# Two attention layers on 8 images: conv weights loaded a head at a time, the closing of a sum moved one unit ahead, first loads of the second pass moved into the first

## The chip, the cores and the metric

One NeuronCore of a Trainium2 chip runs one program that computes both layers for all 8 images. The metric is the time of one execution on the device, in microseconds (us). The kernel before took 4076.93 us, the median of 3 runs (4073.89 to 4082.44). Everything is float32.

## The reference

The input x has shape (8, 256, 64, 64). Layer 0 is an attention whose keys and values come from a 4x4 convolution of stride 4 with a normalization over channels; it runs in the kernel's first pass, and the change touches only where its buffers lie. Layer 1 is a linear attention on several scales, cut here to what matters:

```python
qkv = einsum('oc,bchw->bohw', w_qkv, x)                    # 768 channels
dw  = conv(qkv, w_dw, 5x5, padding 2, one group per channel)
agg = einsum('goi,bgihw->bgohw', w_pw, dw in 96 groups of 8)
ms  = concatenate([qkv, agg], axis=1)                      # 64 heads of 3 x 8 channels
q, k, v = relu(ms[..., :8]), relu(ms[..., 8:16]), ms[..., 16:]   # a column of ones is added to v
kv  = einsum('bhnd,bhne->bhde', k, v)                      # a sum over all pixels
out = einsum('bhnd,bhde->bhne', q, kv);  att = out[..., :-1] / (out[..., -1:] + 1e-15)
result = x + batchnorm(w_proj @ att)
```

## The kernel before, in words

`kernel_body` (L1440) calls three passes one after another; they share DRAM tensors and take their on-chip buffers from pools of their own. Pools of a later pass come to lie over pools of an earlier one, so a first use of a buffer can have to wait for the last use of what lay there. A scheduler orders the instructions of each engine from the program's order and its dependences, and it moves instructions past others where it can. All DMAs are issued by SP, one after another, and an issue that has to wait holds up those behind it.

**First pass** (`first_pass`, L575): layer 0, image by image, and w_qkv of its result. It writes to DRAM: x2 (layer 0's result), planes (qkv cut into grids of even and odd rows and columns), k and v with pixels on partitions, and wt, the 5x5 convolution and w_pw folded into matrices (`conv_weights`, L633).

**Second pass** (`second_pass`, L956): the heads of agg. It has 64 units u = (t, k, b): t of 2 halves, k of 4 groups of heads, b of 8 images, the image innermost, so that eight units in a row use the same weights. Each unit has two convolutions, what = 1 (its output, k, has pixels on partitions) and what = 0 (q, channels on partitions), each of three parts of 16 matmuls (`convolve`, L1070 and L1074). Part 2 comes first; its PSUM bank is copied to "both" by ScalarE (L1077). Parts 0 and 1 are added to "both" by VectorE (s, L1085), and ScalarE makes r by a ReLU (L1086). The matmul operands c come from the grids d by differences (`paired`: VectorE L1012 and L1013, and for what = 1 a copy on POOL, L1016). Further steps:

- `positive` (L1051): ReLU of kq on ScalarE (L1053), and a sum over it on POOL (`reduced`, L1046 to L1048).
- `summed_raw` (L1089): 64 matmuls give the k-by-v sums of the qkv heads in the bank "raw" (L1095). There is one such bank. `ended_raw` (L1138) adds the column for the sum of k by one matmul (L1142), and VectorE copies the bank to mraw (L1144, L1145), which is stored.
- `summed` (L1105): the sums of the agg heads (128 matmuls, L1112), weighted with taps (L1122, L1124) and mixed (L1127 to L1130); `ended` and `spread` bring them into the block form bd.
- `applied` (L1177): ng from r of q and bd, for two parities (L1182), then den (ScalarE L1184, VectorE L1185), tok (L1187), its transpose att (L1194) and the store of att to DRAM (L1196).

The loop runs these for four units at a time, one stage apart: raw and what = 1 of u, sums of u - 1, what = 0 of u - 2, ng of u - 3. In the program's order, `ended_raw(u - 1)` stands between parts 0 and 1 of `convolve(u, 1)`. Loads: grids by `load_cells` (L984, 578 KB each), kq and vq by `load_tokens` (L991, 512 KB; L1001, four of 384 KB), and weights by `load_weights` (L977), 1536 KB in one DMA:

```python
        if now and units[u][2] == 4 and u + 4 < n_all:
            load_weights(u + 4, 1)
        if conv and units[q][2] == 4 and q + 4 < n_all:
            load_weights(q + 4, 0)
```

**Third pass** (`third_pass`, L1246): the qkv heads' own attention and the projection. It loads constants first, the 128x128 mask msk (L1261), vec (L1332) and wproj (L1334); kvm is msk times the stored sums (L1274, L1280); n (L1358), den (L1360, L1361) and tok (L1363), a transpose by matmul (L1376, L1377), the projection p (L1394) of those and of the stored att of the second pass (agg, L1310). raw (L1290) and xs (L1299) are its other loads.

Of the kernel before, what the change touches and what calls it, by code (L numbers as in the profile page):

```python
# [27 lines left out]
F32 = mybir.dt.float32  # L28
# [4 lines left out]
P = 128  # L33
C = 256
# [8 lines left out]
D1 = 8  # L43
# [531 lines left out]
def first_pass(ctx: ExitStack, tc: tile.TileContext, a, fine, planes, x2d, kd, vd, wtd):  # L575
# [3 lines left out]
    const = ctx.enter_context(tc.tile_pool(name="const", bufs=1))  # L579
    nilpool = ctx.enter_context(tc.tile_pool(name="nilpool", bufs=1))  # L580
    xpools = [ctx.enter_context(tc.tile_pool(name=f"xpool{i}", bufs=1)) for i in range(2)]
    two = ctx.enter_context(tc.tile_pool(name="two", bufs=2))
    psum = ctx.enter_context(tc.tile_pool(name="psum", bufs=1, space=bass.MemoryType.PSUM))

    def bank(name):
# [46 lines left out]

    def conv_weights():  # L633
        for j in (2, 3, 0, 1):
            wd = two.tile([P, 16, 6, 16], F32, tag="wd", name=f"wd_{j}", bufs=1)
            nc.sync.dma_start(wd[:, :, :4], a.w_big[:, j].rearrange("p g (n f) -> p g n f", n=4))

            nc.vector.tensor_add(wd[:, :, 4:], wd[:, :, 0:4:2], wd[:, :, 1:4:2])
            for i in range(8):
                w = two.tile([P, 2, 6 * 16, D1], F32, tag="wb", name=f"wb_{j}_{i}", bufs=1)  # L640
                gs = slice(2 * i, 2 * i + 2)
                nc.vector.tensor_tensor(
                    w,
                    wd[:, gs].rearrange("p g n f -> p g (n f)").unsqueeze(3).to_broadcast([P, 2, 6 * 16, D1]),
                    consts["wsmall"][:, j, gs].unsqueeze(2).to_broadcast([P, 2, 6 * 16, D1]),
                    ALU.mult,
                )
                nc.sync.dma_start(wtd[j][:, gs], w.rearrange("p g n o -> p g (n o)"))
                yield
# [3 lines left out]

    def keys_values(b):
        xt = x_tiles[b]
        ln = lambda name: two.tile([P, 2, NK], F32, tag="ln", name=f"{name}_{b}", bufs=3)
        xr = ln("xr")

        ps = psum.tile([P, QB], F32, tag="sr", name=f"sr_{b}").rearrange("p (o k) -> p o k", o=2)
        taps = sorted((phase(dy, dx), dy * R + dx) for dy in range(R) for dx in range(R))  # L660
        for f, tap in taps:
            w = two.tile([P, 2, C], F32, tag="wsr", name=f"wsr_{b}_{f}", bufs=4)
            nc.sync.dma_start(w, a.w_sr[:, :, tap])
            for ci in range(2):
                for oc in range(2):
                    nc.tensor.matmul(  # L666
                        ps[:, oc],
                        w[:, ci, oc * P : (oc + 1) * P],
                        xt[:, ci, f * NK : (f + 1) * NK],
                        start=(f == ci == oc == 0),  # L670
                        stop=(f == R * R - 1 and ci == 1),
                        skip_group_check=True,
                    )
            yield
# [113 lines left out]
    def normed(b, s, c):  # L788
        av, den = sums["av"], sums["den"]
        i = 2 * ((b * NG + s) * 2 + c)  # L790
        att = two.tile([P, QB], F32, tag="att", name=f"att_{b}_{s}_{c}", bufs=4)
        r = two.tile([P, QB], F32, tag="rden", name=f"rden_{b}_{s}_{c}")
        nc.scalar.copy(att, av)
        nc.vector.reciprocal(r, den)  # L794
        nc.vector.tensor_mul(att, att, r)
        nc.scalar.activation(den, den, AF.Copy, accum_out=seen[:, i : i + 1])
        nc.scalar.activation(den, r, AF.Copy, accum_out=seen[:, i + 1 : i + 2])
        return att
# [10 lines left out]


    def new_stage(b, s):
        st = two.tile([P, 4, 2, NB + 1, NB + 1], F32, tag="stage", name=f"stage_{b}_{s}")
        row, col = (0 if s // 4 else NB), (0 if s // 2 % 2 else NB)
        v = st.rearrange("p j f y x -> p (j f) y x")
        nc.gpsimd.memset(v[:, :, row], 0.0)
        nc.gpsimd.memset(v[:, :, :, col], 0.0)
        return st
# [8 lines left out]
    def qkv(b, s, st, j):  # L826
# [16 lines left out]
        if j < 2:  # L843
            return
        if al == 0:
            turned[j] = two.tile([P, NB // 2, 4, D0], F32, tag=f"turned{j}", name=f"turned_{b}_{s}_{j}", bufs=1)
        t = turned[j]
        nc.vector.transpose(  # L848
            t[:, :, 2 * al : 2 * al + 2].rearrange("p y f e -> p f y e"),
# [106 lines left out]
def second_pass(ctx: ExitStack, tc: tile.TileContext, a, planes, kd, vd, wtd, kvd, attd):  # L956
    nc = tc.nc
    B = a.x.shape[0]
    const = ctx.enter_context(tc.tile_pool(name="const2", bufs=1))
    late = ctx.enter_context(tc.tile_pool(name="late2", bufs=2))  # L960

    data = [ctx.enter_context(tc.tile_pool(name=f"data2_{i}", bufs=1)) for i in range(3)]
    two = ctx.enter_context(tc.tile_pool(name="two2", bufs=2))
    psum = ctx.enter_context(tc.tile_pool(name="psum2", bufs=1, space=bass.MemoryType.PSUM))

    def bank(tag, name, bufs=1, n=512):
# [3 lines left out]
    n_all = len(units)  # L970
    wt, grids, cells, kqs, vqs = {}, {}, {}, {}, {}

    def load_weights(u, what):
        t, k, b = units[u]
        pool = data[k % 2 if what else 2]
        w = pool.tile([P, 4, 6 * P], F32, tag=f"w{what}_{k % 2}", name=f"w{what}_{t}_{k}")
        nc.sync.dma_start(w, wtd[2 * what + t][:, 4 * k : 4 * k + 4])  # L977
        wt[t, k, what] = w

    def load_cells(u, what):  # L980
        t, k, b = units[u]
        pool = data[u % 2 if what else 2]
        d = pool.tile([P, 4, (NB + 1) ** 2], F32, tag=f"d{what}_{u % 2}", name=f"d{what}_{u}")
        nc.sync.dma_start(d, planes[b, 2 * what + t][4 * k : 4 * k + 4].rearrange("g p e -> p g e"))  # L984
        grids[u, what] = d.rearrange("p g (y x) -> p g y x", x=NB + 1)


    def load_tokens(u):
        t, k, b = units[u]
        kq = data[u % 2].tile([P, 2, 4, P], F32, tag=f"kq_{u % 2}", name=f"kq_{u}")  # L990
        nc.sync.dma_start(  # L991
            kq.rearrange("p a c e -> p a (c e)"),
            kd[b][4 * t + k].rearrange("a y (m i) b e -> (y m) a (i b e)", i=2),
        )
        kqs[u] = kq
        vq = data[min(u % 3, 1)].tile([P, 4, 6 * P], F32, tag=f"vq_{u % 3}", name=f"vq_{u}")
        v = vd[b][4 * t + k]
        row = (NB2 + 2) * P
        for r in range(4):
            src = [[2 * row, NB], [4 * P, NB // 2], [1, 6 * P]]  # L1000
            nc.sync.dma_start(vq[:, r], bass.AP(tensor=v.tensor, offset=v.offset + r * row, ap=src))  # L1001
        vqs[u] = vq.rearrange("p r (c f h e) -> p r c f h e", c=6, f=4, h=4)
# [2 lines left out]

    def paired(u, what):
        d = grids[u, what]
        pool = two if what else late
        c = pool.tile([P, 2 + what, 4, (NB + 1) * NB // 2], F32, tag=f"c{what}", name=f"c{what}_{u}")
        v = c.rearrange("p n g (y x) -> p n g y x", x=NB // 2)  # L1010
        d0, d1, d2 = (d[:, :, :, i : i + NB - 1 : 2] for i in range(3))
        nc.vector.tensor_sub(v[:, 0], d0, d1)  # L1012
# [3 lines left out]
            nc.gpsimd.tensor_copy(v[:, 2], d1)  # L1016
        cells[u, what] = c

    load_weights(0, 1)
    load_cells(0, 1)  # L1020
    load_tokens(0)

    def load(src, name):
        t = const.tile(list(src.shape), F32, tag=name, name=name)
        nc.sync.dma_start(t, src)
        return t

    load_cells(1, 1)
    load_cells(0, 0)
    load_weights(0, 0)  # L1030
    taps = load(a.w_taps, "taps")
    mix = load(a.w_mix, "mix")
    msk = load(a.mask_h, "msk")
    rep_w = load(a.replicate, "rep_w")
    pix = load(a.pixel, "pix")
    ones = const.tile([P, 1], F32, tag="ones", name="ones")
    nc.vector.memset(ones, 1.0)
    eps = late.tile([P, 1], F32, tag="eps", name="eps", bufs=1)
# [3 lines left out]


    def reduced(u, what, t):
        r = two.tile([P, 4, P], F32, tag=f"red_{what}", name=f"red_{what}_{u}", bufs=1)
# [12 lines left out]
    def convolve(u, what, i):  # L1058
# [14 lines left out]
                        out = out.rearrange("p (y x) -> p y x", y=NB)  # L1073
                    nc.tensor.matmul(out, m, x, start=(da == 0), stop=(da == 1))  # L1074
        if i == 2:
            both = two.tile([P, QB], F32, tag="both", name=f"both{what}_{u}")
# [100 lines left out]
    def applied(u, par):  # L1177
# [2 lines left out]
        pn = bank("ng", f"ng_{u}_{par}", 1, 1024).rearrange("p (h n) -> p h n", h=4)  # L1180
        for h in range(4):
            nc.tensor.matmul(pn[:, h, : P + 16], q[:, par, h], bd[:, h], start=True, stop=True)  # L1182
        den = two.tile([P, 2, 4, 16], F32, tag="den", name=f"den_{u}_{par}")
        nc.scalar.activation(den[:, 0], pn[:, :, P : P + 16], AF.Identity, bias=eps)  # L1184
        nc.vector.reciprocal(den[:, 1], den[:, 0])  # L1185
        tok = two.tile([P, 16, D0], F32, tag="tok", name=f"tok_{u}_{par}")
        nc.vector.tensor_tensor(  # L1187
            tok.rearrange("p f (h e) -> p h f e", e=D1),
            pn[:, :, :P].rearrange("p h (f e) -> p h f e", e=D1),
            den[:, 1].unsqueeze(3).to_broadcast([P, 4, 16, D1]),  # L1190
            ALU.mult,
        )
        att = two.tile([P, 512], F32, tag="att", name=f"att_{u}_{par}")
        nc.vector.transpose(att, tok.rearrange("p f e -> p (f e)"))  # L1194
        c0 = P * t + D0 * k
        nc.sync.dma_start(attd[b][c0 : c0 + D0, par].rearrange("c j n -> j c n"), att)  # L1196
# [2 lines left out]
    for u in range(n_all + 3):  # L1199
# [16 lines left out]
            paired(u + 1, 1)  # L1216
        if now:
            convolve(u, 1, 0)
        if was:
            ended_raw(p)  # L1220
        if now:
            convolve(u, 1, 1)
        if u + 2 < n_all:
            load_cells(u + 2, 1)
# [10 lines left out]
            spread(p)  # L1235
        if conv:
            convolve(q, 0, 1)
        if now and units[u][2] == 4 and u + 4 < n_all:
            load_weights(u + 4, 1)
        if conv and units[q][2] == 4 and q + 4 < n_all:  # L1240
            load_weights(q + 4, 0)

# [338 lines left out]
```

## Time and profile before

| | |
|---|---|
| median of 3 runs | 4076.93 us (4073.89 to 4082.44) |
| the profiled execution | 4078.39 us |
| its span in the profile | 4076.5 us |
| mean granted clock of TensorE | 0.986 |
| first, second, third pass (by TensorE's work) | 0 to 2137, 2137 to 3422, 3422 to 4070 us |
| busy: TensorE, VectorE, ScalarE, POOL | 97%, 47%, 41%, 29% of the span |
| DMA | 691.31 MB, mean 170 GB/s |

The profile is of one execution. Times are counted from the start of its span. A row of a group of instructions gives line, engine, operation and tiles with counts and times. A row of the waits gives the engine, the line that waited, what let it go, and then the sum of the waiting in us, how often, and the longest. A row of the order of time gives start, duration, engine, line and operation; in brackets stands the idle time of the engine before it and what ended it. A table of stretches gives, for each stretch, its length, the busy time of TensorE, its weight loads, VectorE, ScalarE and POOL with the number of instructions, the clock that TensorE was granted, the share of time in which the 16 DMA engines were busy, and GB/s.

### The profile page before, as it was taken

Reading aid. Unit: us, or ns where it says so; the run is one execution under the profiler, and the core shown is the slowest. Engines: PE = TensorE matmul, PEld = TensorE weight load, DVE = VectorE, ACT = ScalarE, POOL = GpSimd, SP = SyncE. Lnnn points to the kernel's source line nnn. Section 1 sums busy time; section 2 is a strip of 40 time slices with the busy share of each in tenths; the row PEclk is TensorE's granted clock in tenths of the full one; section 3 lists DMA queues with packets and bytes.
Section 4 is the critical chain, followed back from the end, with each engine's and each line's share of the span. In section 5 each row is a group of like instructions: output and inputs, shape, how many; then the busy total and the mean of one; then the engine's idle time right before and its main releaser. Section 6 shows DMA issues by size and latency. Waiting matters only on the chain. (4 is left out here: it accounts for less than half of the span.)

```text
span 4076.5 us, 69470 instructions
## 1 busy us (share of the span) xinstructions
PE 3966.0 (97%) x27266; PEld 2328.2 (57%) x27266; DVE 1920.4 (47%) x2724; ACT 1659.5 (41%) x3505; POOL 1196.3 (29%) x1234
## 2 busy tenths in 40 slices
PE   8999999999999999999997899999999998999999
PEld 4433433434334343343336788888888886655655
DVE  2554344343433434434444565565565664444443
ACT  2345455454554545545542222222222223445544
POOL 2233233233332323323333343343343441000000
PEclk9999999999999999999998999999999998999999
DMA  7655435344353444433449777777777766777674
GB/s 234 200 178 158 125 92 150 98 116 133 98 147 102 103 142 105 137 101 101 132 113 257 221 221 225 206 223 230 206 221 221 208 180 172 223 207 228 202 228 138
DMA packets 581408, 691.31 MB, mean 170 GB/s; under 512 B 61392, under 2 KB 430544, under 8 KB 574800
## 3 DMA queue, kind: packets, MB, share of 16 engines
q1 hardware_dynamic: 581072, 686.79, 59.2%
q8 instruction: 216, 3.54, 0.4%
q14 instruction: 120, 0.98, 0.1%
HBM read 412.54 MB, written 274.10 MB: 168 GB/s over the span
## 5 line engine op out<-in xcount | busy, mean ns | idle before, releaser
L781 POOL TENSOR_TENSOR e<-e,e 128x512 f32<-128x512 f32 x512 | 650.0, 1301 | 1206.3 <-PE av L770 1182.7
L794 DVE RECIPROCAL rden<-den 128x512 f32<-128x512 f32 x128 | 429.7, 3357 | 689.8 <-PE den L786 689.8
L829 PE MATMUL qkv<-x,wqkv 128*128 128x512 f32 x1536 | 702.5, 600 | 0.0
L759 ACT ACTIVATE e<-sc 128x512 f32<-128x512 f32 x1024 | 529.3, 603 | 419.2 <-PE sc L753 419.2
L829 PEld LDWEIGHTS qkv<-x,wqkv 128*128 128x128 f32 x1536 | 285.7, 191 | 373.8 <-issue 353.6
L1070 PE MATMUL cv<-w,c 128*128 128x128 f32 x3072 | 404.3, 283 | 12.9 <-POOL c L1016 12.9
L1070 PEld LDWEIGHTS cv<-w,c 128*128 128x128 f32 x3072 | 366.6, 193 | 44.9 <-issue 25.6
L848 DVE STREAM_TRANSPOSE turned<-qkv 128x512 f32<-128x512 f32 x256 | 177.4, 707 | 342.0 <-ACT stage L838 292.8
L753 PE MATMUL sc<-q,kk 32*128 32x512 f32 x2048 | 324.6, 640 | 11.5 <-DVE x L805 8.0
L1086 ACT ACTIVATE r<-s 128x512 f32<-128x512 f32 x256 | 155.8, 629 | 346.2 <-DVE s L1085 346.2
L1412 DVE TENSOR_TENSOR y<-z,xs 128x256 f32<-128x256 f32 x256 | 143.7, 648 | 317.2 <-ACT z L1403 300.8
L770 PE MATMUL av<-e,vv 128*32 128x512 f32 x2048 | 274.5, 608 | 0.0
L838 ACT COPY stage<-qkv 128x512 f32<-128x512 f32 x256 | 149.8, 585 | 306.2 <-PE qkv L829 306.2
L1403 ACT ACTIVATE z<-p,bn 128x256 f32<-128x256 f32 x256 | 133.4, 577 | 317.6 <-PE p L1394 239.4
L1112 PE MATMUL sums<-vq,r 128*32 128x288 f32 x4096 | 261.6, 407 | 0.0
L738 PE MATMUL q<-x,wq 128*128 128x512 f32 x512 | 253.8, 618 | 0.0
L1394 PE MATMUL p<-att,wproj 128*128 128x512 f32 x512 | 249.2, 609 | 4.6 <-ACT att L1377 4.6
L1074 PE MATMUL cv<-c,w 128*128 128x128 f32 x2048 | 253.4, 277 | 0.0
L666 PE MATMUL sr<-x,wsr 128*128 128x256 f32 x1024 | 235.6, 385 | 7.0 <-DMA wsr<-in_w_sr_dram 6.9
L1394 PE MATMUL p<-agg,wproj 128*128 128x512 f32 x512 | 241.7, 595 | 0.0
L1074 PEld LDWEIGHTS cv<-c,w 128*128 128x128 f32 x2048 | 239.7, 192 | 0.0
L1085 DVE TENSOR_TENSOR s<-cv,both 128x512 f32<-128x512 f32 x256 | 172.2, 673 | 140.0 <-PE cv L1070 95.3
(121 smaller groups left out, 4983.9 us busy)
## 6 DMA issues: line engine op xcount, KB each, us to landing
vq<-v SPq DMA_DIRECT2D x256, 384.0 KB
planes<-stage SPq DMA_DIRECT2D x256, 289.0 KB
d<-planes SPq DMA_DIRECT2D x128, 578.0 KB
raw<-planes SPq DMA_DIRECT2D x128, 272.0 KB
x<-in_xp_dram SPq DMA_DIRECT2D x64, 512.0 KB
wsr<-in_w_sr_dram SPq DMA_DIRECT2D x128, 256.0 KB
x<-x SPq DMA_DIRECT2D x128, 256.0 KB
k<-turned SPq DMA_DIRECT2D x256, 128.0 KB
```

The costliest lines, as they stand in the source:

```text
L666: nc.tensor.matmul(ps[:, oc], w[:, ci, oc * P : (oc + 1) * P], xt[:, ci, f * NK : (f + 1) * NK], start=(f == ci == oc == 0), stop=(f == R ...
L738: nc.tensor.matmul(ps, consts["wq"][:, ci, c * P : (c + 1) * P], x_tiles[b][:, ci, s * QB : (s + 1) * QB], start=(ci == 0), stop=(ci == 1),)
L753: nc.tensor.matmul(scs[h], kks[b][rows, c, kc * P : (kc + 1) * P], qs[rows], start=True, stop=True)
L759: nc.scalar.activation(e, scs[h], AF.Exp, scale=D0**-0.5)
L770: nc.tensor.matmul(sums["av"][cols], vvs[b][:, kc, c * P + h * D0 : c * P + (h + 1) * D0], es[h], start=(kc == 0), stop=(kc == 1),)
L781: nc.gpsimd.tensor_tensor(es0[h], es0[h], es1[h], ALU.add)
L794: nc.vector.reciprocal(r, den)
L829: nc.tensor.matmul(ps, consts["wqkv"][:, ci, j * P : (j + 1) * P], x_tiles[b][:, ci, s * QB : (s + 1) * QB], start=(ci == 0), stop=(ci == 1),)
L1070: nc.tensor.matmul(out, x, m, start=(da == 0), stop=(da == 1))
L1074: nc.tensor.matmul(out, m, x, start=(da == 0), stop=(da == 1))
L1112: nc.tensor.matmul(ps[h * D0 : (h + 1) * D0, : 36 * D1].rearrange("p (r n e) -> p r n e", r=3, e=D1), kt[:, par, h, 2 * r + c], vq[:, r : ...
L1394: nc.tensor.matmul(ps.rearrange("p (f q n) -> p f q n", f=4, q=4), wproj[:, j, oc * P : (oc + 1) * P], src, start=(j == 0), stop=(j == 3),)
```

## The change

- **Weights.** `load_weights` gets a head g and loads 384 KB; four calls make up a weight tile. They stand at the end of the loop's body, one per unit of the group before: what = 1 in units b = 0 to 3, what = 0 in units b = 4 to 7.
- **Sum of k.** `ended_raw` is called for the unit u itself and no longer for u - 1.
- **First loads.** The pools of both passes are cut differently. In the first pass, the tiles of `keys_values`, those of `conv_weights` and the rest now have three pools, `keys`, `made` and `rest`. In the second pass, weights, grids, tokens, "both", the sums of `reduced` and taps have pools of their own, placed so that the first weights and taps do not lie over buffers that the first pass uses to its end. den, tok and att move from the pool `two` to `late`. The order of the first loads changes: the first weights of what = 0 and then taps come directly after the first tokens.

The diff, cut to its core (the renamed pools of the first pass left out but for three lines):

```diff
+    keys = ctx.enter_context(tc.tile_pool(name="keys", bufs=1))
     two = ctx.enter_context(tc.tile_pool(name="two", bufs=2))
+    made = ctx.enter_context(tc.tile_pool(name="made", bufs=1))
+    rest = ctx.enter_context(tc.tile_pool(name="rest", bufs=2))
...
-    data = [ctx.enter_context(tc.tile_pool(name=f"data2_{i}", bufs=1)) for i in range(3)]
-    two = ctx.enter_context(tc.tile_pool(name="two2", bufs=2))
+    const, late = pool("const2"), pool("late2", 2)
+    first, second, mid, w_q, third, between, w_taps, two = (
+        pool("first2"), pool("second2"), pool("mid2"), pool("wq2"), pool("third2"), pool("between2", 2),
+        pool("taps2"), pool("two2", 2),
+    )
...
-    def load_weights(u, what):
+    def load_weights(u, what, g):
         t, k, b = units[u]
-        pool = data[k % 2 if what else 2]
-        w = pool.tile([P, 4, 6 * P], F32, tag=f"w{what}_{k % 2}", name=f"w{what}_{t}_{k}")
-        nc.sync.dma_start(w, wtd[2 * what + t][:, 4 * k : 4 * k + 4])
-        wt[t, k, what] = w
+        if g == 0:
+            home = (third if k % 2 else first) if what else (third if k % 2 else w_q)
+            wt[t, k, what] = home.tile([P, 4, 6 * P], F32, tag=f"w{what}_{k % 2}", name=f"w{what}_{t}_{k}")
+        nc.sync.dma_start(wt[t, k, what][:, g], wtd[2 * what + t][:, 4 * k + g])
...
-    load_weights(0, 1)
+    for g in range(4):
+        load_weights(0, 1, g)
     load_cells(0, 1)
     load_tokens(0)
+    for g in range(4):
+        load_weights(0, 0, g)
...
+    taps = load(w_taps, a.w_taps, "taps")
     load_cells(1, 1)
+    mix = load(const, a.w_mix, "mix")
+    msk = load(const, a.mask_h, "msk")
+    rep_w = load(const, a.replicate, "rep_w")
+    pix = load(const, a.pixel, "pix")
     load_cells(0, 0)
-    load_weights(0, 0)
-    taps = load(a.w_taps, "taps")
...
-        den = two.tile([P, 2, 4, 16], F32, tag="den", name=f"den_{u}_{par}")
+        den = late.tile([P, 2, 4, 16], F32, tag="den", name=f"den_{u}_{par}")
...
-        tok = two.tile([P, 16, D0], F32, tag="tok", name=f"tok_{u}_{par}")
+        tok = late.tile([P, 16, D0], F32, tag="tok", name=f"tok_{u}_{par}")
...
-        att = two.tile([P, 512], F32, tag="att", name=f"att_{u}_{par}")
+        att = late.tile([P, 512], F32, tag="att", name=f"att_{u}_{par}")
...
             convolve(u, 1, 0)
-        if was:
-            ended_raw(p)
         if now:
+            ended_raw(u)
             convolve(u, 1, 1)
...
-        if now and units[u][2] == 4 and u + 4 < n_all:
-            load_weights(u + 4, 1)
-        if conv and units[q][2] == 4 and q + 4 < n_all:
-            load_weights(q + 4, 0)
+        if now and u + B < n_all:
+            b = units[u][2]
+            load_weights(u + B - b, 1 if b < 4 else 0, b % 4)
```

More of the change, by code (lines that the diff above doesn't have):

```diff
@@ L634, in conv_weights @@
         for j in (2, 3, 0, 1):
-            wd = two.tile([P, 16, 6, 16], F32, tag="wd", name=f"wd_{j}", bufs=1)
+            wd = made.tile([P, 16, 6, 16], F32, tag="wd", name=f"wd_{j}", bufs=1)
             nc.sync.dma_start(wd[:, :, :4], a.w_big[:, j].rearrange("p g (n f) -> p g n f", n=4))
@@ L639, in conv_weights @@
             for i in range(8):
-                w = two.tile([P, 2, 6 * 16, D1], F32, tag="wb", name=f"wb_{j}_{i}", bufs=1)
+                w = made.tile([P, 2, 6 * 16, D1], F32, tag="wb", name=f"wb_{j}_{i}", bufs=1)
                 gs = slice(2 * i, 2 * i + 2)
@@ L655, in keys_values @@
         xt = x_tiles[b]
-        ln = lambda name: two.tile([P, 2, NK], F32, tag="ln", name=f"{name}_{b}", bufs=3)
+        ln = lambda name: keys.tile([P, 2, NK], F32, tag="ln", name=f"{name}_{b}", bufs=3)
         xr = ln("xr")
@@ L661, in keys_values @@
         for f, tap in taps:
-            w = two.tile([P, 2, C], F32, tag="wsr", name=f"wsr_{b}_{f}", bufs=4)
+            w = keys.tile([P, 2, C], F32, tag="wsr", name=f"wsr_{b}_{f}", bufs=4)
             nc.sync.dma_start(w, a.w_sr[:, :, tap])
@@ L790, in normed @@
         i = 2 * ((b * NG + s) * 2 + c)
-        att = two.tile([P, QB], F32, tag="att", name=f"att_{b}_{s}_{c}", bufs=4)
-        r = two.tile([P, QB], F32, tag="rden", name=f"rden_{b}_{s}_{c}")
+        att = rest.tile([P, QB], F32, tag="att", name=f"att_{b}_{s}_{c}", bufs=4)
+        r = rest.tile([P, QB], F32, tag="rden", name=f"rden_{b}_{s}_{c}")
         nc.scalar.copy(att, av)
@@ L811, in new_stage @@
     def new_stage(b, s):
-        st = two.tile([P, 4, 2, NB + 1, NB + 1], F32, tag="stage", name=f"stage_{b}_{s}")
+        st = rest.tile([P, 4, 2, NB + 1, NB + 1], F32, tag="stage", name=f"stage_{b}_{s}")
         row, col = (0 if s // 4 else NB), (0 if s // 2 % 2 else NB)
@@ L845, in qkv @@
         if al == 0:
-            turned[j] = two.tile([P, NB // 2, 4, D0], F32, tag=f"turned{j}", name=f"turned_{b}_{s}_{j}", bufs=1)
+            turned[j] = rest.tile([P, NB // 2, 4, D0], F32, tag=f"turned{j}", name=f"turned_{b}_{s}_{j}", bufs=1)
         t = turned[j]
@@ L958, in second_pass, with pool @@
     B = a.x.shape[0]
-    const = ctx.enter_context(tc.tile_pool(name="const2", bufs=1))
-    late = ctx.enter_context(tc.tile_pool(name="late2", bufs=2))
-    data = [ctx.enter_context(tc.tile_pool(name=f"data2_{i}", bufs=1)) for i in range(3)]
-    two = ctx.enter_context(tc.tile_pool(name="two2", bufs=2))
+    def pool(name, bufs=1):
+        return ctx.enter_context(tc.tile_pool(name=name, bufs=bufs))
+    const, late = pool("const2"), pool("late2", 2)
[3 more added lines that the diff above has]
+    )
     psum = ctx.enter_context(tc.tile_pool(name="psum2", bufs=1, space=bass.MemoryType.PSUM))
@@ L971, in second_pass @@
     wt, grids, cells, kqs, vqs = {}, {}, {}, {}, {}
-    def load_weights(u, what):
+    def load_weights(u, what, g):
         t, k, b = units[u]
-        pool = data[k % 2 if what else 2]
-        w = pool.tile([P, 4, 6 * P], F32, tag=f"w{what}_{k % 2}", name=f"w{what}_{t}_{k}")
-        nc.sync.dma_start(w, wtd[2 * what + t][:, 4 * k : 4 * k + 4])
-        wt[t, k, what] = w
+        if g == 0:
+            home = (third if k % 2 else first) if what else (third if k % 2 else w_q)
+            wt[t, k, what] = home.tile([P, 4, 6 * P], F32, tag=f"w{what}_{k % 2}", name=f"w{what}_{t}_{k}")
+        nc.sync.dma_start(wt[t, k, what][:, g], wtd[2 * what + t][:, 4 * k + g])
     def load_cells(u, what):
         t, k, b = units[u]
-        pool = data[u % 2 if what else 2]
-        d = pool.tile([P, 4, (NB + 1) ** 2], F32, tag=f"d{what}_{u % 2}", name=f"d{what}_{u}")
+        home = (second if u % 2 else first) if what else third
+        d = home.tile([P, 4, (NB + 1) ** 2], F32, tag=f"d{what}_{u % 2}", name=f"d{what}_{u}")
         nc.sync.dma_start(d, planes[b, 2 * what + t][4 * k : 4 * k + 4].rearrange("g p e -> p g e"))
@@ L989, in load_tokens @@
         t, k, b = units[u]
-        kq = data[u % 2].tile([P, 2, 4, P], F32, tag=f"kq_{u % 2}", name=f"kq_{u}")
+        kq = (second if u % 2 else first).tile([P, 2, 4, P], F32, tag=f"kq_{u % 2}", name=f"kq_{u}")
         nc.sync.dma_start(
@@ L995, in load_tokens @@
         kqs[u] = kq
-        vq = data[min(u % 3, 1)].tile([P, 4, 6 * P], F32, tag=f"vq_{u % 3}", name=f"vq_{u}")
+        vq = (second if u % 3 else first).tile([P, 4, 6 * P], F32, tag=f"vq_{u % 3}", name=f"vq_{u}")
         v = vd[b][4 * t + k]
@@ L1007, in paired @@
         d = grids[u, what]
-        pool = two if what else late
-        c = pool.tile([P, 2 + what, 4, (NB + 1) * NB // 2], F32, tag=f"c{what}", name=f"c{what}_{u}")
+        c = (two if what else late).tile([P, 2 + what, 4, (NB + 1) * NB // 2], F32, tag=f"c{what}", name=f"c{what}_{u}")
         v = c.rearrange("p n g (y x) -> p n g y x", x=NB // 2)
@@ L1017, in paired, with load @@
         cells[u, what] = c
-    load_weights(0, 1)
+    for g in range(4):
+        load_weights(0, 1, g)
     load_cells(0, 1)
     load_tokens(0)
-    def load(src, name):
-        t = const.tile(list(src.shape), F32, tag=name, name=name)
+    for g in range(4):
+        load_weights(0, 0, g)
+    def load(home, src, name):
+        t = home.tile(list(src.shape), F32, tag=name, name=name)
         nc.sync.dma_start(t, src)
         return t
+    taps = load(w_taps, a.w_taps, "taps")
     load_cells(1, 1)
+    mix = load(const, a.w_mix, "mix")
+    msk = load(const, a.mask_h, "msk")
+    rep_w = load(const, a.replicate, "rep_w")
+    pix = load(const, a.pixel, "pix")
     load_cells(0, 0)
-    load_weights(0, 0)
-    taps = load(a.w_taps, "taps")
[L1032 to L1035, printed above, removed]
     ones = const.tile([P, 1], F32, tag="ones", name="ones")
@@ L1044, in reduced @@
     def reduced(u, what, t):
-        r = two.tile([P, 4, P], F32, tag=f"red_{what}", name=f"red_{what}_{u}", bufs=1)
+        r = mid.tile([P, 4, P], F32, tag=f"red_{what}", name=f"red_{what}_{u}", bufs=1)
         nc.gpsimd.tensor_tensor(r, t[0], t[1], ALU.add)
@@ L1075, in convolve @@
         if i == 2:
-            both = two.tile([P, QB], F32, tag="both", name=f"both{what}_{u}")
+            both = between.tile([P, QB], F32, tag="both", name=f"both{what}_{u}")
             nc.scalar.copy(both, ps)
```

## The prediction

> **What bounds the kernel now.** I read the page first, then the waits of TensorE, then a table of stretches, then the order of time around one stall. The head of the page says that TensorE is the bound, and that what can be saved at all is the gap up to the span:
>
> ```profile
> PE 3966.0 (97%) x27266; PEld 2328.2 (57%) x27266; DVE 1920.4 (47%) x2724; ACT 1659.5 (41%) x3505; POOL 1196.3 (29%) x1234
> ```
>
> Span less busy is 4076.5 - 3966.0 = 110.5 us, so an edit that removes no matmul cannot give more than that plus what a lowered clock adds. The table of waits (engine, line waited at, who let it go, us in all, times, longest) tells where the gap lies:
>
> ```profile
> PE raw L1095 <- DVE mraw L1145: 45.4, 9, 8.6
> PE cv L1070 <- POOL c L1016: 12.9, 2, 11.7
> ...
> PE p L1394 <- ACT att L1377: 4.6, 2, 3.4
> PE ng L1182 <- ACT r L1086: 4.3, 1, 4.3
> ...
> PE ng L1182 <- DVE tok L1187: 2.7, 1, 2.7
> ```
>
> Two waits of the second pass hold 58.3 of the 110.5 us. The 45.4 us fall nine times: three at the pass' start, and six in the units in which the weights of the next group are loaded (one in eight). The stretches, cut at unit boundaries (length, busy us and counts of each engine, PE clock, DMA share, GB/s), show a weight unit between two ordinary ones, and the first two units after the start:
>
> ```profile
> 2137.00:2158.60 21.60, 9.29 (x117) 9.04 (x116) 5.95 (x13) 1.75 (x3) 5.26 (x5) 0.68 0.93 284
> ...
> 2238.00:2263.20 25.20, 20.48 (x247) 18.07 (x246) 11.80 (x22) 5.21 (x11) 8.29 (x9) 0.86 0.80 221
> ...
> 2281.80:2300.40 18.60, 18.60 (x247) 16.31 (x246) 11.31 (x22) 5.25 (x10) 7.95 (x9) 1.00 0.74 220
> 2300.40:2327.50 27.10, 20.92 (x248) 18.47 (x246) 11.31 (x22) 6.92 (x13) 8.75 (x10) 0.87 0.70 189
> 2327.50:2346.10 18.60, 18.60 (x247) 16.30 (x246) 11.15 (x22) 3.78 (x8) 6.49 (x9) 1.00 0.74 198
> ```
>
> An ordinary unit is 18.6 us with TensorE never idle. The weight unit is 8.5 us longer, only 6.2 us of them idle; the other 2.3 us are the same matmuls at a lower clock. Why it stalls is in the order of time of the later weight unit, first SP's issues, then VectorE (start, duration, the idle time before it in brackets):
>
> ```profile
> 2451.47 0.52 SPq L977 DMA_DIRECT2D w<-wt  x1
> 2456.81 0.52 SPq L1196 DMA_DIRECT2D att<-att  x1
> 2457.43 2.17 SPq L984 DMA_DIRECT2D d<-planes  x2
> ```
>
> ```profile
> 2466.36 0.73 DVE L1012 TENSOR_TENSOR c<-d 128x544 f32<-128x544 f32 x1 [7.58 <-DMA d<-planes]
> ...
> 2472.69 0.17 DVE L1144 COPY mraw<-raw 128x32 f32<-128x32 f32 x1
> 2472.79 0.14 DVE L1145 COPY mraw<-raw 128x1 f32<-128x1 f32 x1
> ```
>
> The 1536 KB of weights go out ahead of the unit's two grids d. SP then stands at an att store that waits for VectorE, so the grids go out 6.4 us after kq (2.3 us in an ordinary unit) and land behind the weights. VectorE stands 7.58 us at the first use of a grid (1.25 us in the unit before); ten operations queue behind it (among them den and tok of L1185 and L1187), and then the two copies of raw's bank. The single raw bank is thus free at 2472.8, and TensorE, next in its order raw of the following unit, stood 4.39 us. The other weights, what = 0, go out after the att store and ahead of vq only; there no stall follows.
>
> **What the Trainium skill says.** "DMA: Bandwidth & Descriptors", Queues, rings and completion order: SP owns one row of rings, and each DMA engine consumes descriptors in ring order. So a 1.5 MB load holds what is issued behind it; the 7.58 us agree. The same page, Bandwidth: 1 MB moves at 341 GB/s. The trace is slower: 247 to 303 GB/s where the share is 0.9 or more. I use 280. "TensorE: Matmul & The Clock Gate", Part 1: after an idle window of about 3.4 us the clock is halved until a busy window has passed. This agrees: after the 4.39 us stall the granted clock is 0.73 and then 0.77 over 14 us, 1.00 before and after.
>
> **The change part by part.** What I cost is the order that the changed program has on each engine, which the diff alone doesn't show. The sum is against the profiled execution: span 4076.5 plus 1.9 us outside, 4078.4, which is 1.5 us above the median of 4076.9.
>
> *Weights by the head, and the sum of k in its own unit.* The six weight units measure 25.90, 26.83, 24.01, 26.33, 26.02 and (the one in the table) 27.06 us, against 18.63: 7.27+8.20+5.38+7.70+7.39+8.43 = 44.4 us. In the changed order the pieces are not one to a unit: they go out as soon as a slot is free, of what = 1 two (786 KB) ahead of the grids and two after them. So the grids lie behind 786 KB instead of 1573 KB, 2.8 us at 280 GB/s, and are no longer behind the att store. That alone would leave perhaps 1.5 us of each stall. But the copies of raw's bank now lie in the unit of their own sum, and the next raw comes a whole block of sums later: it can't wait for VectorE's lateness. What is late next is tok at L1187, which ng of the other parity needs: even in the stalled unit tok was done at 2471.4, about when TensorE, without the stall, would come to it (2471.9). With earlier grids there is room. I take 0.5 us left per unit, 3 in all, between 0 and 3 each: -41.4. The extra issues, 18 more of about 0.5 us per eight units on SP at most, hide behind 149 us in which SP mostly waits; uncovered they would be 4 us a group.
>
> *kq earlier.* kq is now issued at a unit's start, ahead of vq. Its ReLU on ScalarE (1.06 us) now stands in front of "both" of part 1. In the trace a kq lands about 7.5 us after its issue (it waits 3.3 us for it, 56 times); from 0.9 us after the unit's start this is 8.4, "both" is wanted at 6.2 to 6.7, but TensorE only needs the chain behind it at 14, so that landing up to 10 is free. I take 0, between 0 and 1 us per unit.
>
> *First weights and taps in the first pass.* Start excess over 18.63 per unit: the third, fourth and fifth unit are 20.57, 29.96 and 25.22 (1.9+11.3+6.6), with 1.1 of idle ahead of them: 21.0 us. Its DMA share is 0.9 to 1.0: the start is short of bandwidth. About 4.1 MB (taps 1.2, what = 0 weights 1.6, a grid 0.6, half the next weights 0.8) go out in the first pass now, where the DMA share is 0.4 to 0.5: 14.6 us of transfer at 280 GB/s out of the jam. The wait of 11.7 us for the first c stays: it is for the last planes to be written. I leave 6 of 21, between 1 and 14: -15. The first pass itself: taps, weights and new pools cost TensorE nothing in the built order (same matmuls, same order), as 2.7 MB hide under a share below a half; uncovered, a few us. I take +0.5 (0 to 4).
>
> *Second to third pass.* The pools are laid out anew. The third pass' constants now lie over den, tok and att, so the load of msk waits until the very last att store has landed. Before, it was issued at 3401.03 and landed at 3410.0, 9.0 us later. The last store was issued at 3422.77; the wait of VectorE for msk (5.26 us) and of TensorE (4.34) that it caused go, so the last store comes some 3 to 5 us earlier, 3418 to 3420, lands 2 to 3 later, msk lands 5 to 9 after that, behind 0.5 to 1 MB of other loads, and then kvm (0.5) and n can start: 3426 to 3437, against 3422.14 now. Of the loss of 4 to 15 the wait at p (3.43) and a little more comes back, since the loads behind are long there. I take +8.5 (+2 to +14).
>
> Sum: -41.4 - 15 + 0.5 + 8.5 = -47.4; with a clock that is a little lower after the boundary's gap, +1: -46.4. 4078.4 - 46.4 = **4032**, 1.1% under the median.
>
> **Rivals.** *A, a new wait takes part of the place.* The bytes are the same, and clumps of two pieces still go out ahead of the grids. If VectorE's c stays 5 us late, ng waits for tok in each of six units: 3 us of idle and 2 of clock, 30 in place of the 3 above: 4032 + 27 = 4059. For: DMA share 0.95 where a w goes out. Against: tok was in time even at 7.58 us lateness. *B, it goes better.* No residual stalls, start clean, boundary +3: 4078.4 - 44.4 - 20 + 3 = about 4017. *C, slower: the ReLU of kq.* ScalarE takes its queue in order; a kq that lands later than 10 us after the unit's start holds "both", then s, r and the sums, and TensorE loses each us past that point in all of some 57 units, covering weight units or not. The gain of 46 is eaten at 0.8 us per unit, and 0.2% slower from 0.95: landing from about 11.0, ten us after issue instead of 7.5. At 12 it is 57 x 2 = +114 - 46 = +68, about 4146. For: vq's 1.5 MB in the same queue. Against: vq is issued behind it. *D, the change doesn't do what it says*: one head a unit is indeed not what the order shows; but what stalls is the place before the grids, so this is priced in A.
>
> **How the numbers follow.** Forecast (4022 to 4046) 0.60, A 0.16, B 0.14, C 0.06, and 0.04 for a wash in which boundary and start eat the rest. Faster by over 0.2% (8 us, about what a measurement can tell from no change) holds forecast, A and B: 0.89. Within: 0.05; slower: 0.06. The range takes in B's middle and A's, and leaves out C, the wash and the outer halves of those two: 4012 to 4060. Within it lies some 0.8.
>
> **What would show it.** Right: the waits lose raw <- mraw but for one or two at the start; weight units are 18.6 to 19.5 us; cv <- POOL c stays near 12; the first n comes 8 us or so later behind msk, with a wait on kvm of 5 us or more in TensorE's list. Wrong: a new line ng <- tok or ng <- r with six or more counts (A, C), ScalarE's idle at kq above 4 us with TensorE's after it (C), sr or sc waits in the first pass grown, or a boundary that costs over 14 us.

## The result and the profile after

The changed kernel took 4088.4 us, the median of 4 runs (4084.15 to 4092.29), against 4076.07 of the kernel before beside it: ratio 1.0027, 95% interval 1.001 to 1.0045. It is slower by 12 us; 4032 was forecast. The profiled execution of the changed kernel took 4092.29 us with a span of 4090.5, that of before 4078.39 and 4076.5. Cut at the last qkv matmul of the first pass and at the first sums of units 5 and 63, the two spans compare so (us):

| stretch | before | after | difference | forecast |
|---|---|---|---|---|
| first pass, to its last qkv matmul | 2136.3 | 2139.5 | +3.2 | +0.5 |
| start of the second pass, units 0 to 4 | 126.9 | 116.2 | -10.7 | -15 |
| units 5 to 62 (58 units) | 1125.3 | 1141.4 | +16.1 | -41.4 |
| the rest | 688.1 | 693.5 | +5.4 | +9.5 |
| span | 4076.5 | 4090.5 | +14.0 | -46.4 |

(The first row spreads from 2131.9 to 2139.5 over the profiles of this study, so +3.2 is no finding.) The third row holds nearly the whole error. First the head of the page of the changed kernel, then its waits of TensorE:

```profile
PE 3953.8 (97%) x27266; PEld 2346.9 (57%) x27266; DVE 1889.1 (46%) x2724; ACT 1651.9 (40%) x3505; POOL 1166.5 (29%) x1234
```

```profile
PE cv L1084 <- ACT both L1087: 63.9, 48, 5.5
PE n L1366 <- issue: 17.7, 1, 17.7
PE cv L1080 <- POOL c L1024: 12.0, 1, 12.0
```

The 45.4 us of raw <- mraw are gone, as forecast. In their place stands a wait at "both" that the forecast didn't have, 48 times instead of 9. The stretches, a weight unit and the two units after it:

```profile
2293.90:2318.00 24.10, 19.72 (x264) 17.85 (x252) 11.48 (x24) 5.74 (x11) 8.53 (x11) 0.93 0.80 239
2318.00:2336.50 18.50, 18.45 (x260) 16.59 (x250) 10.34 (x22) 4.52 (x9) 6.07 (x8) 1.00 0.68 182
2336.50:2356.05 19.55, 18.53 (x271) 16.70 (x258) 10.90 (x23) 5.12 (x10) 7.40 (x11) 1.00 0.94 276
```

A weight unit is still 24.1 us (24.1 to 25.7 for the six), and now ordinary units wait too: here the second of the two, of 19.55 us, with 1.0 us of it idle. What they wait for is in the order of time of an ordinary unit (raw has ended at 2356.2, just ahead of it): SP, then ScalarE, then TensorE.

```profile
2352.20 2.94 SPq L993 DMA_DIRECT2D d<-planes  x2
2355.63 1.09 SPq L1206 DMA_DIRECT2D att<-att  x1
2356.82 1.76 SPq L1000 DMA_DIRECT2D kq<-k  x1
2360.18 2.51 SPq L1010 DMA_DIRECT2D vq<-v  x4
```

```profile
2367.49 1.06 ACT L1063 ACTIVATE kq<-kq 128x1024 f32<-128x1024 f32 x1 [10.05 <-DMA kq<-k]
2368.45 0.57 ACT L1087 COPY both<-cv 128x512 f32<-128x512 f32 x1
```

```profile
2366.73 0.28 PE L1161 MATMUL few<-ones,red_agg 128*128 128x1 f32 x2
2369.07 3.02 PE L1084 MATMUL cv<-d,w 128*128 128x128 f32 x16 [2.06 <-ACT both L1087]
```

kq goes out 0.6 us after raw has ended and lands 10.7 us later, which is when its ReLU starts. ScalarE stands at its ReLU for 10.05 us, and "both", whose input TensorE finished at 2362, stands behind it. That is the forecast's rival C. At the end of the second pass, SP, VectorE and TensorE in this order:

```profile
3432.05 0.55 SPq L1206 DMA_DIRECT2D att<-att  x1
...
3439.66 0.35 SPq L1269 DMA_DIRECT2D msk<-in_mask_dram  x1
```

```profile
3442.27 0.29 DVE L1282 TENSOR_TENSOR kvm<-msk,kva 128x128 f32<-128x128 f32 x1 [2.44 <-DMA msk<-in_mask_dram]
```

```profile
3442.81 4.18 PE L1366 MATMUL n<-kvm,q 128*128 128x144 f32 x16 [17.69 <-issue]
```

This is the chain that was forecast, longer than forecast: n waits 17.7 us for kvm, kvm for msk, msk for the last att store (SP stands 3.4 us at the issue of msk until that store has landed).

### The profile page after: what moved, and what is told of

It is laid out like the page before. It is cut to its first block, busy times and chain, and to the rows that moved or that the text cites. A ratio compares the mean times of both kernels' runs of the same rounds, so it can differ in the third digit from the quotient of the medians.

```text
span 4090.5 us, 69544 instructions
## 1 busy us (share of the span) xinstructions
PE 3953.8 (97%) x27266; PEld 2346.9 (57%) x27266; DVE 1889.1 (46%) x2724; ACT 1651.9 (40%) x3505; POOL 1166.5 (29%) x1234
## 5 line engine op out<-in xcount | busy, mean ns | idle before, releaser
L1080 PE MATMUL cv<-w,c 128*128 128x128 f32 x3072 | 385.3, 279 | 12.0 <-POOL c L1024 12.0
L1063 ACT ACTIVATE kq<-kq 128x1024 f32<-128x1024 f32 x64 | 67.6, 1057 | 541.8 <-DMA kq<-k 445.6
```

The source lines that it names most:

```text
L1080: nc.tensor.matmul(out, x, m, start=(da == 0), stop=(da == 1))
```

## The experiments

Theory 1: closing raw in its own unit sets raw of the next unit free to go to the unit's end; the ReLU of kq then comes ahead of "both" on ScalarE, and kq lands too late for it. Theory 2: the pieces of weights make the queue late. Each kernel ran beside the kernel before; ratios have 95% intervals.

**Which part of the change it is.** `only_raw` is the kernel before with this alone:

```diff
             convolve(u, 1, 0)
-        if was:
-            ended_raw(p)
         if now:
+            ended_raw(u)
             convolve(u, 1, 1)
```

> The kernel before, with nothing changed but that the sum of k is closed in its own unit. Theory 1 (the moved ending lets raw of the next unit go to the unit's end; with it the ReLU of kq moves ahead of the copy 'both' of part 1 on ScalarE, waits there for kq's transfer, and holds the PSUM bank that the first part of the other convolution needs): the wait cv <- ACT both appears here too, 40 to 90 us in all, raw <- mraw is gone, and the time is 4085 to 4110. Theory 2 (the ending is harmless; the weights in pieces ahead of kq make it late): no such wait worth over 10 us, and about 4030 us, since the six stalls at raw are gone.

4117.4 us, ratio 1.0099 (1.0082 to 1.0116), slower than both theories had it. The wait at "both" is there without any piece of weights, and one at ng behind it:

```profile
PE cv L1074 <- ACT both L1077: 59.9, 39, 5.8
PE ng L1182 <- DVE tok L1187: 35.1, 10, 4.9
```

`undo_raw` is the changed kernel with the same edit turned round.

> The changed kernel with the ending of raw put back to the following unit; weights by the head, pools and first loads stay changed. Theory 1: the wait cv <- ACT both is gone (under 5 us), units are 18.6 us again, the six weight units cost 0 to 5 us each, the loss at the start of the third pass stays; 4025 to 4050 us. Theory 2: the wait stays, as the weights in pieces are what delays kq; 4075 us or more.

4029.2 us, ratio 0.988 (0.9863 to 0.9896). Units 5 to 62 take 1081.7 us, 18.65 each, weight units included. Its line at raw:

```profile
PE raw L1105 <- DVE mraw L1155: 6.2, 3, 4.6
```

So with raw's ending in its old place, the rest of the change leaves 6.2 of the 45.4 us at raw, nearly all of it at the start of the pass, and the moved ending costs 59 us. Theory 2 falls.

**Is it the late kq, and only through the ReLU?** `kp` gives the ReLU a tile of its own. The buffer of kq is then free as soon as the ReLU has read it, and the next load goes out a unit sooner.

```diff
-        nc.scalar.activation(kq, kq, AF.Relu)
-        reduced(u, "raw", (kq[:, 0], kq[:, 1]))
+        kp = two.tile([P, 2, 4, P], F32, tag="kp", name=f"kp_{u}", bufs=1)
+        nc.scalar.activation(kp, kq, AF.Relu)
+        kqs[u] = kp
+        reduced(u, "raw", (kp[:, 0], kp[:, 1]))
```

> The changed kernel with the ReLU of kq written to a tile of its own, so that the buffer of kq comes free a unit sooner and its load goes out a unit sooner; the order on TensorE and ScalarE stays. Theory 1: kq has landed when the ReLU comes up, the wait cv <- ACT both is under 10 us in all, ordinary units are 18.3 to 18.4 us; 4000 to 4020 us. Rival (the queue as a whole is late, and kq is only the one that shows): the wait goes to another tile, and the time stays within 25 us of 4088.

4007.1 us, ratio 0.9829 (0.9813 to 0.9845). No line of "both" is left in the waits of TensorE, and units 5 to 62 take 1063.8 us, 18.34 each. Of the 77.5 us that the changed kernel takes longer there, TensorE stands idle for 57, and it is busy for 20 more: its granted clock is 0.985 there, and 1.00 in `kp`. The stretches of the unit that took 27.1 us before, and of the next, have no gap:

```profile
2283.00:2301.30 18.30, 18.30 (x256) 16.52 (x252) 11.57 (x23) 5.46 (x10) 7.92 (x9) 1.00 0.90 262
2301.30:2319.70 18.40, 18.40 (x262) 16.62 (x254) 11.67 (x23) 5.46 (x10) 7.93 (x9) 1.00 0.80 231
```

`norelu` leaves the ReLU of kq out, so that the sums are of unrectified keys, and leaves every load at its place in SP's queue:

```diff
-        nc.scalar.activation(kq, kq, AF.Relu)
```

> The changed kernel with the ReLU of kq left out (so the sums of the qkv heads are of unrectified keys); the loads of kq stay where they are and as late as they are. Theory 1 (ScalarE's order is what hurts: a late kq harms only through the ReLU that stands ahead of both): the wait cv <- ACT both is under 10 us in all, and the time is 4000 to 4020 us, as with kq's load a unit earlier. Rival (late kq and weights hurt by themselves, through raw or through the grids behind them): 4040 us or more.

4007.3 us, ratio 0.9833 (0.9816 to 0.9849), units 5 to 62 in 1064.0 us. In 13 of the 56 units with a load of kq it still lands more than 9.2 us after the unit's start, the first matmul of its sums; in the changed kernel that is late enough for a wait (worked out in the section on why the prediction was wrong). Here TensorE loses nothing by it. So a late kq harms through the ReLU's place on ScalarE. In most units, though, kq is also less late here, which matters below.

**Is the PSUM bank what makes it bite so early?** In the changed kernel the part that waits takes the bank that "both" is copied from, some 2 us earlier in the unit than ng, which I had named as the first to need that chain. `four_banks` gives the parts a fourth bank:

```diff
-        ps = bank("cv", f"cv{what}_{u}_{i}", 3)
+        ps = bank("cv", f"cv{what}_{u}_{i}", 4)
...
-        ps = bank("sums", f"sums_{u}")
+        ps = sums[u] = bank("sums", f"sums_{u}")
...
-        few[u] = bank("few", f"few_{u}")
+        few[u] = sums.pop(u)[:, 320:]
```

> The changed kernel with a fourth PSUM bank for the convolutions' parts, won by putting the small results of 'few' into free columns of the bank of sums; loads and the place of the ReLU stay as they are. Theory 1 in its finer form (TensorE is held at the fourth part after both's own, since that part takes both's bank): the wait cv <- ACT both is gone, the next thing held is ng <- tok three us later in the unit, where only the weight units and a few others still stop, 10 to 35 us in all; 4020 to 4050 us. Rival (the bank is not the limit, s and r behind both are): the same waiting shows at ng or at sums, and the time is 4075 us or more.

4088.9 us, ratio 1.0024 (1.0016 to 1.0031): nothing gained. This theory of mine falls.

```profile
PE ng L1192 <- DVE tok L1197: 64.5, 47, 4.5
```

The wait only moved. The two ways round are nearly as long: in the changed kernel from the ReLU's start to the waiting part 1.6 us (2346.90 to 2348.49), and from there to raw's end 7.7 (2356.19), 9.3 in all; with four banks 3.3 and 5.7, 9.0 in all.

**Why kq is late.** From issue to ReLU, where ScalarE waits for kq, the median is 6.9 us before and 9.65 after. Before, kq went out ahead of the unit's grids; after, it goes out right behind them, two grids and an att store (1.4 MB), the first of which goes out 4.1 us ahead of kq in the median (4.6 in the unit shown). `kq_scalar` also issues it when raw has read the buffer, but from ScalarE's queue:

```diff
-        nc.sync.dma_start(
+        nc.scalar.dma_start(
             kq.rearrange("p a c e -> p a (c e)"),
```

> The changed kernel with the load of kq issued by ScalarE, right ahead of its ReLU, at the same point of the unit (after raw has read the buffer), so that it stands in another queue than the grids and att stores that SP has just issued. Theory 1 (kq is late because some 1.4 MB stand ahead of it in SP's ring): kq lands 2 to 5 us after its issue sooner than the 9 to 10 us of the changed kernel, the waits at both fall below 25 us, 4020 to 4060 us. Rival (the DMA engines' load is the limit whatever the queue): landing and waits stay, within 12 us of 4088 or slower.

4011.4 us, ratio 0.9842 (0.9826 to 0.9858), more than theory 1 had. The median from issue to ReLU is 7.1 us:

```profile
2359.20 0.37 ACTq L1000 DMA_DIRECT2D kq<-k  x1
2365.89 1.06 ACT L1063 ACTIVATE kq<-kq 128x1024 f32<-128x1024 f32 x1 [6.14 <-DMA kq<-k]
```

So the DMA engines can carry kq in time, and issuing it from another engine cures the kernel. But 7.1 against 9.65 us is not the work of the queue alone: here, where TensorE doesn't wait, the first grid goes out 5.6 us ahead of kq in the median, and not 4.1. `norelu` is the better comparison. It has kq in SP's queue and no wait at "both" either, and the first grid goes out 5.5 us ahead:

```profile
2349.82 1.99 SPq L993 DMA_DIRECT2D d<-planes  x2
2355.29 0.36 SPq L1000 DMA_DIRECT2D kq<-k  x1
```

Its kq has landed 7.3 us after issue in the median, and 6.0 to 10.8 (counted to the last of the 16 completion marks that the trace holds for each load). In units without weights ahead of kq, and with the first grid 5.3 to 5.6 us ahead, the two queues hardly differ: 6.96 us from SP, 6.91 from ScalarE in the median, though the latest takes 9.64 from SP and 7.51 from ScalarE. In the six weight units it takes 9.6 to 10.6 from SP and 7.6 to 8.7 from ScalarE. So the queue decides how late the late ones are. The rest of the 9.65 us comes with the wait itself, since `norelu` has the same loads in the same queue. The likely link is that the wait brings the grids nearer to kq; no run here changes that distance alone.

The Trainium skill, "DMA: Bandwidth & Descriptors", Queues, rings and completion order, says that each DMA engine takes turns between the rows that have work, which agrees with the weight units. The same page, Issuing engines are not separate DMA queues, says that issuing on several engines will only save the time of the sequencer; here it saved some 2 us of a transfer that had weights ahead of it and 77 us of the kernel's time, and the measurement decides.

**What the pieces are worth.** `whole_w` is the changed kernel with `load_weights` moving four heads in one DMA, called where it was before:

```diff
-        nc.sync.dma_start(wt[t, k, what][:, g], wtd[2 * what + t][:, 4 * k + g])
+        nc.sync.dma_start(wt[t, k, what][:, g : g + n], wtd[2 * what + t][:, 4 * k + g : 4 * k + g + n])
...
```

> The changed kernel with each group's weights in one load of 1536 KB again, at the places in the loop that the kernel before had; all else stays changed. Theory 1: ordinary units are as in the changed kernel, and in the weight units kq comes later by the bytes that now stand ahead of it: 2 to 4 us more in each of six, 4090 to 4115 us. Rival (it is the pieces ahead of kq and their issues that make kq late in all units): the wait cv <- ACT both falls below 30 us, and the time below 4070 us.

4113.7 us, ratio 1.0095 (1.0078 to 1.0112). `kp_whole` is the same edit on `kp`:

> The cure of kq's ReLU (a tile of its own) on the changed kernel with weights in one load of 1536 KB again. If the weights by the head matter by themselves, the weight units cost 1 to 4 us each here and nothing with pieces: 4012 to 4030 us. If the six stalls of the kernel before were cured by the freed raw bank alone, 4003 to 4011 us, as with pieces.

4009.2 us, ratio 0.9822 (0.9806 to 0.9838). Where kq's ReLU is the bound, pieces are worth 25 us; with that cured they are worth nothing that can be measured (4007.1 against 4009.2, spreads overlapping), so where raw's ending is moved and the ReLU is out of the way, the six stalls are gone without pieces too. `raw_kp` puts `only_raw` and `kp` together, without pieces, new pools or moved loads:

> The kernel before with the sum of k closed in its own unit and the ReLU of kq in a tile of its own; weights whole, pools and first loads as before. Theory 1: ordinary units are 18.35 us, the wait at raw and the wait at both are gone; the start keeps its jam (10 us more than with the first loads moved), the third pass starts as before (5 us less), the weight units as in the run with whole weights: 4010 to 4035 us. Rival (the gain comes from the pieces and the moved loads): 4050 us or more.

4012.2 us, ratio 0.9833 (0.9817 to 0.985). The moved ending and a ReLU out of the way are thus worth all but 5 of the 71 us by which `kp` is faster than the kernel before; the rest of the change is small beside them.

**The start of the third pass.** `tail` puts den, tok, att and eps in the pool `two`:

```diff
-        den = late.tile([P, 2, 4, 16], F32, tag="den", name=f"den_{u}_{par}")
+        den = two.tile([P, 2, 4, 16], F32, tag="den", name=f"den_{u}_{par}")
...
```

> The changed kernel with den, tok, att and eps of the second pass back in the pool 'two', so that the third pass' constants lie over c of what = 0 instead; all else stays changed. Theory 1: the load of msk waits for the last convolution instead of for the last att store, the first n starts 10 to 16 us sooner, and the gap of 17.7 us ahead of it is under 8; 4070 to 4079 us. Rival (the loads of raw and xs queued ahead of msk set n, or a later wait takes the gain back): under 5 us gained.

4106.4 us, ratio 1.0073 (1.0056 to 1.0089): a miss, and the experiment was not clean. The edit moved the addresses of all later pools, and the first weights now go out only behind the first pass' last stores (2143.6 to 2156.3 us; in the changed kernel the last of them at 2131.4). The start took 133.8 us instead of 116.2 and units 5 to 62 8 us more, while what comes after took 6.6 less. `split` keeps the addresses, and with them the short start (114.5 us):

```diff
-    const, late = pool("const2"), pool("late2", 2)
+    const, late, last = pool("const2"), pool("late2", 2), pool("last2", 2)
...
-        den = late.tile([P, 2, 4, 16], F32, tag="den", name=f"den_{u}_{par}")
+        den = last.tile([P, 2, 4, 16], F32, tag="den", name=f"den_{u}_{par}")
...
```

> The changed kernel with eps, den, tok and att of the second pass in a pool of their own right behind c of what = 0, so that no address of any tile moves but that of eps; the first loads stay in the first pass. The load of msk then waits for the last convolution instead of the last att store. Theory: from the last sums to the first n it is 34 us instead of 45.8, of which the third pass gives some 5 back, all else as in the changed kernel: 4078 to 4084 us. Rival (the slower units of the run with den, tok and att in 'two' came with the boundary and not with the addresses): 4095 us or more.

4087.4 us, ratio 1.0023 (1.0012 to 1.0035), between the two cases and a miss. The first n comes 34.9 us after the start of the last sums instead of 45.8, and nothing is won: the waits of TensorE of this kernel show where it went.

```profile
PE at L1384 <- DVE tok L1371: 9.0, 2, 7.2
...
PE n L1366 <- ACT q L1331: 6.6, 1, 6.6
```

n now waits for q, and the next step for tok of the third pass, which VectorE can't write before the second pass' att store has left the buffers under it (5.46 us at L1371). `kp_split` has both cures:

> The changed kernel with both cures: the ReLU of kq written to a tile of its own, and eps, den, tok and att in a pool of their own. If the two costs are independent, the gain of the second (5 to 9 us) adds to the 4007 us of the first: 3997 to 4003 us. If the wait at the third pass' start was hiding other loads of that pass, under 3 us come of it.

4005.6 us, ratio 0.9827 (0.981 to 0.9843): 1.5 us under `kp`, within the spread of either. The gains don't add; the second cure is worth under 3 us, as the other of the two expectations had it.

## Why the prediction was wrong, step by step

- **Which wait goes: right.** raw <- mraw is gone wherever raw is closed in its own unit, and in `kp` the six weight units are 18.4 us. Either half of the change would have done it: in `undo_raw` it is gone from the weight units with the ending in its old place, in `raw_kp` without pieces.
- **"kq earlier ... I take 0, between 0 and 1 us per unit": this is the step that failed.** Changed kernel against `kp`, units 5 to 62 cost 77.5 us, 1.34 per unit, beyond the upper end. I took kq's landing, about 7.5 us after issue (the median is 6.9), from a place where the grids go out behind it, and costed its move past vq only. It was also moved behind the two grids. From issue to ReLU it is 9.65 us now, and what is free ends sooner. I had TensorE at ng 14 us after the unit's start, as in the kernel before (13.8), but raw no longer stands ahead of ng, which comes at 12.9 in `kp`. A unit without waits is 18.35 us, and the next unit starts 9.14 us after the ReLU where the ReLU is late, so it may start 9.2 us after the unit's start, where I had set 10. In the changed kernel it starts at 9.96 in the median: 9.96 + 9.14 = 19.1 us, the median of the units. The six weight units bring the mean to 19.68.
- **It recurs, because it is a loop.** The load of kq waits for raw to have read its buffer, and raw of the next turn comes at the end of the chain that waits for kq. In such a loop lateness isn't absorbed later; each unit pays it. It also feeds on itself: in `norelu`, with the same loads in the same queue but no wait, kq lands 7.3 us after issue in the median, which would be in time.
- **Weight units.** In the changed kernel three pieces stand ahead of kq there, kq goes out 2.2 to 2.8 us after the unit's start instead of 0.2, and the ReLU waits up to 12.9 us for it. So the stall that the change removes from raw came back at "both", 24.1 to 25.7 us a unit.
- **Rival C** had mechanism and place, at a chance of 0.06. It put the point from which the kernel is slower at about 11 us after the unit's start. By the measured terms, the units may grow by what start and rest give, to (1125.3 + 10.7 - 5.4) / 58 = 19.5 us each, before the whole is slower. From the ReLU to the next unit's start it is 9.5 us in the mean, the lowered clock included, so that point lies near 10.0 us after the unit's start; the ReLU starts at 10.2 in the mean. It said "Against: vq is issued behind it", and left out the grids ahead.
- **Start: right in kind, 10.7 us gained instead of 15.** The wait for the first c stayed, 12.0 us. The rate of 247 to 303 GB/s that I worked with left out a busy stretch: from 2150.0 to 2158.6 us the kernel before moved 397 GB/s.
- **Second to third pass: right.** A gap of 17.7 us ahead of n, but over the whole rest +5.4 us against +9.5 with the clock's term. `split` shows why so large a gap costs so little: what stands behind it waits for other things of the same time.
- **The gain of raw at the unit's end** was missed: a unit is 18.34 us in `kp` and 18.65 in `undo_raw`, some 18 us over 58 units. In the unit of `undo_raw` at 2541.7 us raw falls between matmuls 14 and 15 of a convolution part and adds 0.89 us there; ahead of the sums, in the unit of `kp` at 2539.1, it adds 0.62.

## What to carry to other kernels

When an edit lets a scheduler move a load, cost it from what stands ahead of it at its new place in the queue, not from the latency at its old one. Follow the engine that waits for it: if its queue is in order, what stands behind the wait is late too, and if the load's own start hangs on the end of that chain, every turn pays. A landing time measured while something waits can itself be in part an effect of the wait. A dependence on a buffer (here one of 4 KB per partition for the ReLU's result) can be worth more than the transfers around it.

## What the runs showed of the hardware that I had not expected

A load of 512 KB behind two loads of 578 KB and a store in the same queue landed 7.0 us after its issue in the median where the first of them had gone out 5.3 to 5.6 us ahead (`norelu`), and 9.7 us where it was 4.0 to 4.15 (changed kernel), both in units without weights ahead. With weights of the same queue ahead of it, it took 9.6 to 10.6 us, and from another engine's queue 7.6 to 8.7.

TensorE's clock fell once after a wait shorter than the 3.4 us that the prediction counts with: in the changed kernel a wait of 2.06 us that ended at 2369.07 was followed by a granted clock of 0.50 from 2370.1 to 2373.5. After one of 2.17 us that ended at 2845.13 it stayed at 1.00.

And moving den, tok and att, some 9 KB per partition, from one pool to another made the kernel 18 us slower (`tail`), and not so with the same pools at unmoved addresses (`split`).
